# Four transfers of a turned score unit: one block of keys from all 128 partitions in place of a quarter of the queries from 32

## The chip, the cores and the metric

The kernel runs on one core of a Trainium2 chip. It is measured in device microseconds of one execution: the median of three runs before the change is 1908.62 us (1905.71 to 1908.88). Instructions go to five engines, each with its own queue in order: PE (matmuls, with weight loads PEld beside them), DVE, ACT, POOL, and SP, which here does nothing but issue transfers. All transfers are carried by the core's 16 DMA engines.

## The reference

A gated cross attention is followed by a gated mixture of experts. With x of 32 x 112 x 256 and a context of 32 x 375 x 256, all float32:

```python
lat = layer_norm(_layernorm(x))          # 112 queries a batch
kv_input = concat([layer_norm(ctx), lat])# 375 + 112 = 487 keys
q, k, v = lat @ Wq, *split(kv_input @ Wkv)   # 16 heads of 64
attn = softmax(q k^T / 8)
x = x + tanh(g_xattn) * ((attn v) @ Wout)
gate = top 2 of 8 of softmax(xf @ gate_w), made to add up to 1
x = x + tanh(g_ffn) * sum over the two of gate * (gelu(xf @ w1 + b1) @ w2 + b2)
```

What matters here is the middle: every softmax matrix (112 queries x 487 keys, one for each of 32 x 16 heads) is computed with the queries on the partitions, and the product with v needs it with the keys on the partitions.

## The kernel before

The attention goes by units. A unit is one batch and two pairs of heads, that is four score matrices of 128 x 487; there are 128 units, and two of them (two batches, the same heads) make a period, of which there are 64 (the loop over `n` in steps, two to a period).

Each unit lies in one of three SBUF tiles `exs` of 128 partitions x 2048 floats (8 KB a partition, 1 MB in all). A partition is a query: 128 of them, as four groups `a` of 32. A partition's 2048 floats are four blocks `k` of 512 floats, and a block holds, for both pairs, four chunks of keys and both heads, 32 keys `r`: key number c * 128 + k * 32 + r.

The way of a unit, with its lines:

- `scores` (L536) multiplies q and k into PSUM banks, DVE takes the row maxima (L546), and `exps` (L555) writes the exponentials from ACT into the unit's `exs` tile. As there are three tiles, unit n + 3 is written over unit n, once that one has been sent.
- `norm` (L566, L569) divides by the sums, on ACT, and `turn_blocks` (L574) turns every 32 x 32 square in place on DVE, once for each pair.
- Squares are now turned, but still stand where they stood. `send_blocks` (L580) writes the unit to a DRAM tile `turned` of four blocks k x 32 rows x four groups a x 512 floats, in four transfers issued by SP, 256 KB each. In DRAM the squares stand in the order that the product needs.
- `take_blocks` (L587) reads the whole of `turned` back in one transfer of 128 partitions x 8 KB into `exT`, of which there are two buffers. It waits on SP for the four transfers of its unit.
- `attend` (L600) multiplies v and `exT` on PE, and ACT takes the result out of PSUM (L617).

The order is written out by hand, for every engine alike (a manual schedule, with a small table `PLAN` for ten places of a period). In the first half of a period SP issues, at the second of five places, the two reads of `exT` for the units that were sent a period ago; at the fourth place it issues the four transfers of the next period's first unit, and at the second place of the late half those of its second unit. `attend` of a period stands at the start of the next one. Between them SP issues all else: loads of x and of the context (`load`, L274 and L278; a context tile goes in two transfers, of 112 and of 13 rows), pieces of the expert weights that are summed ahead (`piece_in`, `piece_out`, L1375 to L1419), rows of the output (L651). SP works in order: a transfer that has to wait holds all that stand behind it.

After the 64 periods come the experts (`hidden_pair`, `second_pair`, `run`), which don't use `turned`.

Of the kernel before, what the change touches and what calls it, by code (L numbers as in the profile page):

```python
# [23 lines left out]
def kernel(  # L24
# [59 lines left out]
    KTB, EXB, ETB = 4, 3, 2  # L84
# [18 lines left out]
    QB, QW, Q = 4, 32, S // 4  # L103
# [17 lines left out]
    turned = [dram.tile([QB, QW, QB, 2 * NCK * 2 * QW], F32, name=f"turned_{n}") for n in range(4)]  # L121
# [70 lines left out]
    if True:  # L192
# [313 lines left out]
        exs = [const.tile([P, QB, 2, NCK, 2, QW], F32, name=f"ex_{n}") for n in range(EXB)]  # L506
# [68 lines left out]

        def send_blocks(n, eng=nc.sync):


            for a in range(QB):
                eng.dma_start(  # L580
                    turned[n % 4][:, :, a, :].rearrange("k j n -> j k n"),
                    exs[n % EXB][a * QW : (a + 1) * QW].rearrange("j k q c h r -> j k (q c h r)"),
                )

        def take_blocks(n):
# [938 lines left out]
        norm(1, 0)  # L1524
        turn_blocks(0, 1)
        send_blocks(0)
        units[0, 1][6]()
        norm(1, 1)
        turn_blocks(1, 0)
        weight_sums(0, 2)  # L1530
        units[0, 1][1]()
        turn_blocks(1, 1)
        send_blocks(1)
        units[1, 0] = seven(1, 0, 0)
        for kv, k in PROLOGUE:
# [17 lines left out]
        for n in range(LAST):  # L1553
# [17 lines left out]
            def step(what, period=period, beside=beside, qn=qn):  # L1571
                s, p = int(what[1]), int(what[-1])
                if what[0] == "q":
                    for j in qn:
                        q_unit(j // NG, j % NG + NG * s)
                elif what[0] in "kv":
                    at = beside[what[0]]
                    if at[1] < (UNITS, UNITS // 2)[at[0]]:
                        if at not in units:
                            units[at] = seven(*at)  # L1580
                        units[at][p - 1]()
                elif period + 1 < UNITS:
                    s += 2 * (period + 1)
                    if what[0] == "n":
                        norm(s, p)
                    elif what[0] == "t":
                        turn_blocks(s, p)
                    else:
                        send_blocks(s)
# [24 lines left out]
            k = n - 44  # L1614
# [116 lines left out]
        r, _ = route_parts(g, nc.vector)  # L1731
# [130 lines left out]
```

## Time and profile before

| | |
|---|---|
| median of three runs | 1908.62 us (1905.71 to 1908.88) |
| the profiled execution: its own time | 1907.72 us |
| its span, first to last instruction | 1905.9 us |
| PE busy | 1876.3 us, 98% of the span |
| DVE, ACT, POOL busy | 1353.5, 1136.4, 992.5 us |
| SP's transfers, packet time as a share of 16 engines | 73.6%, 413.31 MB |
| transfers of L580: first and last issue | 34.0 and 1468.8 us, 512 of 256 KB |
| reads of `exT`, L587 | 128 of 1024 KB |

The profile tells of one execution. Each instruction has a start and a duration; a wait is put down to the semaphore that came last. "DMA share" is the mean busy share of the 16 DMA engines, "GB/s" what they moved together; the one by the other gives the rate at which a busy engine works. The transfers' packets are recorded with their sizes but without the number of the engine that carried them. A transfer's landing shows as increments of its semaphore; how many increments each transfer gave can be counted in the trace, between its issue and the next wait for the same semaphore.

### The profile page before, as it was taken

What the parts mean: (1) busy time and instruction counts of PE and PEld (TensorE: products, weight loads), DVE (VectorE), ACT (ScalarE), POOL (GpSimd) and SP (SyncE); (2) the same over time, 40 slices, a digit from 0 to 9 for tenths busy, and PEclk for the clock granted to TensorE, in tenths of its full rate; (3) what the DMA queues carried; (4) which work ended last, traced back from release to release, by engine and by line L of the source; (5) the groups of instructions that cost most, each with busy time, mean ns of one, the idle gap of its engine ahead of it and who ended that gap; (6) DMA issues with size and microseconds to landing.
All of it is one profiled execution on the core that took longest, in us unless ns stands there. A gap on an engine that the chain in (4) does not pass through costs nothing. (4 is left out here: it accounts for less than half of the span.)

```text
span 1905.9 us, 38258 instructions
## 1 busy us (share of the span) xinstructions
PE 1876.3 (98%) x12560; PEld 1433.5 (75%) x12560; DVE 1353.5 (71%) x2868; ACT 1136.4 (60%) x2718; POOL 992.5 (52%) x1475
## 2 busy tenths in 40 slices
PE   8999999999999999999999999999999999999998
PEld 4667777677777676777676777677677999999887
DVE  6787878787877878787878787878776477844111
ACT  5767666666776666667766666666756334434333
POOL 6433333435445746585556655753334588877212
PEclk9999999999999999999999999999999999999999
DMA  7777766767788888798979898896668786897872
GB/s 202 193 229 209 214 196 198 205 182 205 226 227 265 253 246 251 230 280 250 271 224 284 233 268 242 252 265 195 198 184 256 244 240 180 245 336 232 231 205 46
DMA packets 261049, 433.23 MB, mean 227 GB/s; under 512 B 30728, under 2 KB 149072, under 8 KB 244464
## 3 DMA queue, kind: packets, MB, share of 16 engines
q1 hardware_dynamic: 247232, 413.31, 73.6%
q0 software_dynamic: 11328, 15.33, 4.2%
q10 hardware_dynamic: 2288, 2.12, 0.4%
q8 instruction: 101, 1.65, 0.3%
q14 instruction: 100, 0.82, 0.1%
HBM read 301.37 MB, written 172.28 MB: 249 GB/s over the span
## 5 line engine op out<-in xcount | busy, mean ns | idle before, releaser
L555 ACT ACTIVATE ex<-bank,nmx 128x512 f32<-128x512 f32 x512 | 343.6, 697 | 85.7 <-DVE nmx L546 85.2
L569 ACT ACTIVATE ex<-ex,rc 128x512 f32<-128x512 f32 x512 | 342.7, 721 | 76.1 <-DVE rc L566 75.4
L546 DVE TENSOR_REDUCE nmx<-bank 128x1 f32<-128x487 f32 x512 | 298.6, 655 | 85.9 <-PE bank L536 83.6
L574 DVE STREAM_TRANSPOSE ex<-ex 128x1024 f32<-128x1024 f32 x256 | 314.9, 1230 | 19.5 <-ACT ex L569 15.7
L487 POOL TENSOR_TENSOR vv<-tmpv,vv 128x512 f32<-128x512 f32 x64 | 82.1, 1282 | 404.1 <-ACT vv L475 403.4
L536 PE MATMUL bank<-kT,qTs 64*128 64x487 f32 x1024 | 236.3, 588 | 3.0 <-DVE kvT L365 1.7
L600 PEld LDWEIGHTS bank<-exT,vv 128*64 128x64 f32 (+1 forms) x4096 | 198.9, 137 | 30.9 <-issue 22.6
L600 PE MATMUL bank<-exT,vv 128*64 128x112 f32 (+1 forms) x4096 | 213.0, 261 | 2.3 <-DMA exT<-turned 1.6
L617 ACT COPY outT<-bank 128x256 f32<-128x256 f32 (+3 forms) x160 | 40.0, 314 | 263.9 <-PE bank L600 258.8
L434 PE MATMUL bank<-tT,wkv_s 128*128 128x487 f32 x378 | 186.3, 575 | 0.5 <-ACT ex L555 0.5
L439 PE MATMUL bank<-wkv_s,tT 128*128 128x256 f32 x768 | 186.7, 379 | 0.0
L439 PEld LDWEIGHTS bank<-wkv_s,tT 128*128 128x128 f32 x768 | 144.8, 190 | 43.3 <-issue 21.4
L1164 POOL DMA_INDIRECT out_dram<-y,xs x60 | 93.5, 1558 | 154.0 <-DVE y L1191 77.9
L536 PEld LDWEIGHTS bank<-kT,qTs 64*128 64x128 f32 x1024 | 98.8, 187 | 99.2 <-issue 69.9
L1405 POOL TENSOR_TENSOR piece<-piece 128x128 f32<-128x128 f32 x256 | 116.9, 457 | 89.7 <-DMA piece<-in_L_ffn_w_dram 78.3
L439 PE MATMUL bank<-wkv,kvT 128*128 128x256 f32 x512 | 132.0, 380 | 0.8 <-ACT ex L555 0.6
L439 PEld LDWEIGHTS bank<-wkv,kvT 128*128 128x128 f32 x512 | 94.6, 190 | 50.5 <-issue 33.9
L484 DVE TENSOR_TENSOR kT<-bank,kT 128x487 f32<-128x487 f32 x189 | 120.8, 640 | 14.0 <-POOL kT L487 7.5
L434 PE MATMUL bank<-kvT,wkv 128*128 128x487 f32 x252 | 130.1, 598 | 0.0
L484 DVE TENSOR_TENSOR vv<-bank,vv 128x512 f32<-128x512 f32 x192 | 128.2, 668 | 1.8 <-POOL vv L487 0.2
L1219 ACT ACTIVATE h<-h,b 128x256 f32<-128x256 f32 x160 | 66.1, 495 | 91.9 <-DVE h L1230 53.2
L373 PEld LDWEIGHTS bank<-kvT,wq_sb 128*128 128x128 f32 x512 | 96.2, 188 | 28.9 <-issue 17.0
(296 smaller groups left out, 3718.2 us busy)
## 6 DMA issues: line engine op xcount, KB each, us to landing
turned<-ex SPq DMA_DIRECT2D x512, 256.0 KB
exT<-turned SPq DMA_DIRECT2D x128, 1024.0 KB
w<-in_L_ffn_w_dram SPq DMA_DIRECT2D x132, 256.0 KB
w_s<-ws SPq DMA_DIRECT2D x80, 256.0 KB
w_t<-ws SPq DMA_DIRECT2D x80, 256.0 KB
w_b2x<-in_L_ffn_w_dram SPq DMA_DIRECT2D x38, 512.0 KB
ws<-piece SPq DMA_DIRECT2D x64, 256.0 KB
cin<-in_ctx_dram SPq DMA_DIRECT2D x32, 336.0 KB
```

The source lines that it names most:

```text
L373: nc.tensor.matmul(ps, lhsT=wq_sb[:, k, i * P : (i + 1) * P], rhs=kvT[g][:, k, :, SC:NK], start=(k == 0), stop=(k == KD - 1),)
L434: nc.tensor.matmul(ps, lhsT=w[:, 0, i * P : (i + 1) * P], rhs=x[:, :NK], start=True, stop=True)
L439: nc.tensor.matmul(ps[:, c, :], lhsT=x[:, (2 * h + c) * P : (2 * h + c + 1) * P], rhs=w[:, 1, i * P : (i + 2) * P], start=True, stop=True,)
L484: nc.vector.tensor_tensor(v[o], ps, v[r], ALU.add)
L536: nc.tensor.matmul(ps[:, :NK], lhsT=qT[b // 2, i][r, b % 2].rearrange("p a i -> p (a i)"), rhs=kT[b, i][r, :], start=True, stop=True,)
L546: nc.vector.tensor_reduce(nmx[b, i][:, j : j + 1], pss[b, i][j][:, :NK], AX.X, ALU.max, negate=True)
L555: nc.scalar.activation(exs[n % EXB][:, :, p, :, j, :], ps[j].rearrange("p (c k r) -> p k c r", c=NCK, r=QW), AF.Exp, bias=nmx[b, i][:, j : ...
L569: nc.scalar.mul(t, t, rc[:, j : j + 1])
L574: nc.vector.transpose(t, t)
L600: nc.tensor.matmul(ps[y * DH : (y + 1) * DH, r, x * S : (x + 1) * S].rearrange("p (a i) -> p a i", a=QB), lhsT=vv[j // 2, c // 2][:m, c % ...
L1164: add = nc.gpsimd.indirect_dma_start(out=outf, out_offset=bass.IndirectOffsetOnAxis(ap=xs[t][:, b, D + 1 : D + 2].bitcast(I32), axis=0), i ...
L1405: nc.gpsimd.tensor_tensor(o, l, r, op) for o, l, r, op in ops
```

## The change

`send_blocks` still issues four transfers of 256 KB from SP, at the same place and behind the same waits. Before, transfer `a` carries the 32 partitions of group a whole, four blocks of 2 KB from each. Now transfer `k` carries one block of 2 KB from each of 128 partitions. What lies in DRAM at the end is the same, and so is `take_blocks`.

```diff
         def send_blocks(n, eng=nc.sync):
 
-
-            for a in range(QB):
+            for k in range(QB):
                 eng.dma_start(
-                    turned[n % 4][:, :, a, :].rearrange("k j n -> j k n"),
-                    exs[n % EXB][a * QW : (a + 1) * QW].rearrange("j k q c h r -> j k (q c h r)"),
+                    turned[n % 4][k].rearrange("j a n -> a j n"),
+                    exs[n % EXB][:, k].rearrange("p q c h r -> p (q c h r)"),
                 )
```

In the built program a transfer before has the counts 32 x 4 x 512 on both sides. After, the SBUF side counts 128 rows of 512, and the DRAM side 4 x 32 x 512: the outermost count is the group a, with 512 floats from one to the next, then the row j. One line fewer stands in the file, so all lines behind L578 have numbers that are smaller by one. The order of the instructions of every engine is the same in both programs.

## The prediction

> **What bounds the kernel now.** I read the page's busy times first, then its slices, then the attention stage alone, then what SP waits for.
>
> ```profile
> PE 1876.3 (98%) x12560; PEld 1433.5 (75%) x12560; DVE 1353.5 (71%) x2868; ACT 1136.4 (60%) x2718; POOL 992.5 (52%) x1475
> ...
> DMA  7777766767788888798979898896668786897872
> ...
> q1 hardware_dynamic: 247232, 413.31, 73.6%
> ```
>
> PE is busy for 98% of the span, in all forty slices. The DMA row is the second thing to see: 60 to 90% of all sixteen engines' time is taken in nearly every slice, so transfers have cover, but not much.
>
> The windows of the trace, first the whole stage in which L580 is issued, then three short stretches (columns: stretch, length, busy time of PE, PEld, DVE, ACT, POOL, clock, DMA share, GB/s):
>
> ```profile
> 34.00:1470.00 1436.00, 1430.30 (x9103) 1018.04 (x9101) 1130.83 (x2345) 958.66 (x2273) 725.31 (x1139) 1.00 0.80 231
> 56.00:57.50 1.50, 1.50 (x10) 1.33 (x9) 1.50 (x4) 1.38 (x4) 0.77 (x1) 1.00 0.99 198
> 58.50:59.50 1.00, 1.00 (x20) 0.88 (x20) 1.00 (x2) 0.82 (x2) 0.92 (x2) 1.00 0.99 291
> 48.00:49.50 1.50, 1.50 (x9) 1.32 (x8) 0.90 (x3) 1.50 (x7) 0.00 (x0) 1.00 0.97 410
> ```
>
> In the stage PE lacks 1436 - 1430.3 = 5.7 us, and the clock is granted in full. The 64 periods take 1436 / 64 = 22.4 us each, and a DMA engine is busy for 0.80 x 22.4 = 17.9 us of that: 4.5 us are free. The short stretches give the rate of one busy engine (GB/s / 16 / share). At 56 us only one quarter of a unit is on its way out at a time: 12.5 GB/s. At 58.5 us, with several quarters in flight, 18.4. At 48 us only `exT` comes in: 26.4. The whole stage has 18.0.
>
> SP's own waits in that stage, and its order in one period:
>
> ```profile
> SPq L580 <- DVE ex L574: 545.5, 89, 12.6
> SPq L587 <- DMA turned<-ex: 41.3, 33, 2.7
> ```
>
> ```profile
> 624.65 2.86 SPq L580 DMA_DIRECT2D turned<-ex  x4
> 627.61 1.45 SPq L1419 DMA_DIRECT2D ws<-piece  x1
> 629.61 4.23 SPq L580 DMA_DIRECT2D turned<-ex  x4
> ...
> 638.37 0.92 SPq L587 DMA_DIRECT2D exT<-turned  x2
> ...
> 645.93 3.06 SPq L580 DMA_DIRECT2D turned<-ex  x4
> ```
>
> SP waits for DVE, so sends leave as soon as their unit is turned; the reads wait 41.3 us in all for the sends to land. The sends have landed about when SP comes to the reads, 638.37 - 633.84 = 4.5 us after the last of eight was issued.
>
> **The change, part by part.**
>
> *How many engines carry a transfer.* This decides all. A transfer's semaphore must go up by 16. Counted in the trace, the 13-row loads of the context (L278) go up in 14 steps in 29 of 32 cases, and the four 2-row loads at the start (L1428) in 3 steps: one for each row, and one step for what is missing. Transfers whose outermost count is 32 (L580), 64, 112 or 128 go up in 16. So engines get whole entries of the outermost dimension, and with fewer than 16 entries fewer engines work. The new transfer has 4 there on the DRAM side, 128 on the SBUF side; no row of before has two different counts. I take the smaller: a group a is one entry and can't be cut, so four engines carry the transfer, each one group, 32 packets of 2 KB. I also take it that they are the same four each time; no row tells.
>
> The Trainium skill, page "DMA: Bandwidth & Descriptors", section "Why a DMA increments its semaphore by 16 and not by 1", says it outright: as many engines, 16 at most, as divide the outermost counts of both sides, and from SP the lowest-numbered ones. By it the new transfers all run on engines 0 to 3. Against it stands "SBUF — State Buffer", section "Door 1: The DMA port swizzle": 32 partitions reach 8 of 16 ports and 128 reach all. The row at 56 us agrees (198 GB/s with every engine busy, against 410); were that all, a unit would leave in about half the time, and the sum would be rival 1's 1906 us; by the first page it is the 2959 us below. The 13-row load decides between them here.
>
> *The busiest engines.* In a period two units leave, 8 x 262,144 bytes = 2.10 MB; a quarter of it, 524 KB, now goes through each of the four engines, where it was 131 KB. At 26.4 GB/s that is 19.9 us, at 12.5 GB/s 41.9 us. I take 18.4 GB/s, 28.5 us: the stretch at 58.5 us is nearest, as there more than one quarter is read at once, which the four engines will do too, each in a quarter of its own, two at a time in partitions that may get in each other's way.
>
> *All else on these engines.* The stage moves 231 GB/s x 1436 us = 332 MB, of which 512 x 0.262 = 134 MB are sends. The other 198 MB are spread over sixteen engines: 193 KB an engine and period. At 26.4 GB/s 7.3 us, at the stage's mean of 18.0 10.7 us; I take the middle of the rates, 22 GB/s, 8.8 us, as the twelve other engines get out of the way.
>
> *Where the queue runs dry.* SP issues the second read of `exT` only when the second unit of the period before has landed, and behind this read stand the loads, the pieces and the next sends. The first read, which waits for the first unit alone, covers some of that. Least 0; at most 4 us, about the 4.5 us that pass now between the last send and the reads; I take 1.5, an estimate nearer to the lower end since the first read is queued already.
>
> *The waits that this makes.* Three: the reads on SP (L587), longer by what the four engines are late; with them all that SP has behind them. ACT's exponentials (L555) of unit n + 3, which are written over unit n, now wait for a transfer. Behind that wait stand ACT's copies out of PSUM (L475, L617) and `norm` (L569), which DVE's `turn_blocks` and so the next sends need. PE's scores and products come behind those: the 22.4 us of compute are cover for the DMA engines up to 22.4 us and no further. Four engines with 28.5 + 8.8 + 1.5 = 38.8 us a period are the bound. PE then idles for 16.4 us in each.
>
> *Costed at nothing.* SP issues as many instructions; each may take longer for its new shape (the 512 took 407 us in all, 0.8 us each). SP waited 545.5 us for DVE, which hides even half as much again. DVE, ACT, POOL and PE do the same work. The experts after 1470 us send nothing of the kind.
>
> *Sum.* 64 x (38.8 - 22.4) = 1050 us on the profiled execution: span 1905.9 + 1050 = 2956, its time 1907.7 + 1050 = 2958; it lay 0.9 us below the median of the runs, so 2959. With all lower ends 19.9 + 7.3 + 0 = 27.2 us a period, 1908.6 + 64 x 4.8 = 2216; with all upper ends 41.9 + 10.7 + 4 = 56.6 us, 4097.
>
> **The rivals.**
>
> 1. *Sixteen engines after all.* If the 128 rows of the SBUF side set the number, all sixteen work, and their rate moves from 12.5 towards 26.4 GB/s. The mechanism is a send in half the time, at L580, and what it can give back is what PE lacks in the stage, 5.7 us, so 1903; more likely 2 or 3 us of it, 1906, since the longest wait of PE there is 1.7 us and for DVE. For it: the row at 56 us. Against it: the 13-row and 2-row loads. It decides from the point where each of the four has 16 steps. This is the case on the other side.
>
> 2. *Four engines, but another four for each transfer.* Then every engine carries one group of one block, as many bytes as before; a transfer takes 32 packets in a row where it took 8 (at 12.5 GB/s 5.2 us in place of 1.3), but four run beside each other. The reads have 4.5 us before SP comes to them, so at most a microsecond a period comes through, and PE's order has most of a period to spare: 1905 to 1920. Nothing in the rows of before speaks for or against it.
>
> 3. *Four engines, and the pairs out of each other's way.* The engines read different partitions and stay apart: 26.4 GB/s, 19.9 + 8.8 + 1.5 = 30.2 us, 1908.6 + 64 x 7.8 = 2408. For it: a busy engine can do 26.4. Against: this is the rate of reads of 8 KB a row, and the sends have 2 KB.
>
> 4. *Four engines in step.* 12.5 GB/s throughout: 41.9 + 8.8 + 1.5 = 52.2 us, 3816. For it: the row at 56 us. Against: there all sixteen draw on the same 32 partitions.
>
> **How the numbers follow.** My forecast, four fixed engines at a rate in between, 0.65; rival 3 0.15; rival 4 0.07; rival 1 0.08; rival 2 0.05. The range leaves out rivals 1, 2 and 4 (0.20) and holds the others, 50 us or so wider than rival 3 below, and above to a period of 48.2 us: 2350 to 3560. The forecast's own range, at 22 and at 15 GB/s, is 23.8 + 10.3 = 34.1 and 35.0 + 10.3 = 45.3 us a period: 2657 to 3374. A change under 0.2%, 4 us, can't be told from none. Slower: 0.87 of the four-engine cases and 0.01 of rival 2; same: 0.04 and 0.04 of rivals 2 and 1; faster 0.04. Even at all lower ends a four-engine case is 300 us slower.
>
> **What would show it.** Right: each L580 transfer's semaphore goes up in few steps, 4 and one, not 16; in the stage the DMA share falls to about four tenths ((28.5 / 4 + 8.8) / 38.8) and the bytes to 332 MB / 2483 us = 134 GB/s; SP waits for turned<-ex at L587 by hundreds of microseconds; ACT L555 waits for a transfer; PE's share is near 63%. Wrong: 16 steps and PE at 98% (rival 1), or few steps and the old time (rival 2). A busiest engine that isn't the bound would show as PE waits that don't repeat every period.

## The result, and the profile after

The changed kernel takes 2391.8 us (median of four runs, 2383.7 to 2402.4) against 1908.3 us (now the median of four runs of the kernel before): 1.254 times the time before, 95% interval 1.249 to 1.259. The forecast was 2959 us in a range of 2350 to 3560: the right side and the right bound, but a loss of 1050 us where it is 484. Rival 3, with 2408 us, is the one that came.

The profiled execution took 2383.7 us. Its page, the parts of busy times, slices and queues:

```profile
span 2381.9 us, 38258 instructions
PE 2027.8 (85%) x12560; PEld 1528.4 (64%) x12560; DVE 1359.6 (57%) x2868; ACT 1145.5 (48%) x2718; POOL 988.5 (41%) x1475
...
DMA  5544444444455555565555555555544567689783
...
q1 hardware_dynamic: 241088, 413.28, 51.7%
```

PE is down from 98% to 85%, and the DMA engines are less busy than before, 4 to 5 tenths in the attention, while the kernel is slower. Nothing in the sixteen engines' mean looks like a bound. The windows show what is hidden in that mean (stretch, length, busy times of the five engines, granted clock, DMA share, GB/s); first the stage, then two stretches in which sends are under way, in the second alone, in the first with a few other packets:

```profile
34.00:1952.00 1918.00, 1587.06 (x9124) 1117.13 (x9123) 1139.32 (x2355) 968.23 (x2274) 722.89 (x1145) 0.92 0.52 174
816.00:818.00 2.00, 2.00 (x28) 1.92 (x24) 0.62 (x2) 0.00 (x0) 1.77 (x3) 0.60 0.27 104
848.00:850.00 2.00, 2.00 (x25) 2.00 (x23) 1.46 (x3) 0.00 (x0) 1.80 (x4) 0.50 0.26 102
```

A share of 0.26 is four engines of sixteen (0.25) and a little. SP issued four sends between 810.53 and 814.74 us and four more from 817.54 us on, so several are queued at once; if each went to engines of its own, the share would be near 1. They all stand in line for the same four. The rate of one busy engine is 104 / 16 / 0.27 = 24.1 GB/s in the one stretch, 24.5 in the other.

Two counts in the trace say the same. Every one of the 512 sends makes its semaphore go up in 5 steps, four and one; before, 464 of 512 counted 16 up to the next issue on the same semaphore, and the rest fewer, as that issue came between. And of the 1919 us from the first send to the end of the last, fewer than four packets are under way in 25 us, exactly four or five in 1051 us: the four engines are hardly ever short of work. The 65,536 packets of 2 KB of the sends took 1434 us for each of four engines, 22.4 us a period; what is left of the 1919 us, 485 us or 7.6 us a period, is a remainder: all other traffic on these engines, and the little time in which they had nothing to do. Together 30.0 us a period, where it was 22.4.

That it is the same four each time, and not a queue that carries one send after the other, shows in transfers that run on all sixteen engines. The loads of the weights' pieces (L1374, 63 of 64 seen with all 16 steps) have twelve steps by 3.7 us after their issue and the last four at 6.0 to 8.7 us, in the median; before, the sixteen came evenly between 3.5 and 5.4 us. So four engines are late with their shares and twelve are not.

The waits, SP's and then all engines', and PE's first group:

```profile
SPq L586 <- DMA turned<-ex: 354.7, 117, 8.9
```

```profile
POOL piece L1404 <- DMA piece<-in_L_ffn_w_dram: 428.9, 29, 23.4
...
ACT ex L555 <- DMA turned<-ex: 141.3, 44, 5.7
PEld bank L599 <- DMA exT<-turned: 135.1, 63, 6.1
PE bank L599 <- DMA exT<-turned: 124.9, 65, 5.4
```

All three waits that were forecast are there: SP in front of the reads (41.3 us before), ACT in front of an `exs` tile that is not yet sent, and PE behind the reads. POOL's wait for the weights' pieces, 78.3 us before, shows the same: a quarter of each of these transfers goes through the four.

### The profile page after: what moved, and what is told of

Read it like the earlier page. It is cut to its first block, busy times and chain, and to the rows that moved or that the text cites. A ratio compares the mean times of both kernels' runs of the same rounds, so it can differ in the third digit from the quotient of the medians.

```text
span 2381.9 us, 38258 instructions
## 1 busy us (share of the span) xinstructions
PE 2027.8 (85%) x12560; PEld 1528.4 (64%) x12560; DVE 1359.6 (57%) x2868; ACT 1145.5 (48%) x2718; POOL 988.5 (41%) x1475
## 5 line engine op out<-in xcount | busy, mean ns | idle before, releaser
L599 PE MATMUL bank<-exT,vv 128*64 128x112 f32 (+1 forms) x4096 | 286.9, 308 | 135.6 <-DMA exT<-turned 124.9
L599 PEld LDWEIGHTS bank<-exT,vv 128*64 128x64 f32 (+1 forms) x4096 | 259.9, 168 | 179.7 <-DMA exT<-turned 135.1
L439 PE MATMUL bank<-wkv,kvT 128*128 128x256 f32 x512 | 152.9, 426 | 84.9 <-ACT ex L555 84.8
L434 PE MATMUL bank<-tT,wkv_s 128*128 128x487 f32 x378 | 193.8, 596 | 32.9 <-ACT ex L555 32.9
L439 PE MATMUL bank<-wkv_s,tT 128*128 128x256 f32 x768 | 212.6, 419 | 1.4 <-ACT ex L555 1.4
L439 PEld LDWEIGHTS bank<-wkv,kvT 128*128 128x128 f32 x512 | 101.4, 210 | 154.0 <-ACT ex L555 121.5
L439 PEld LDWEIGHTS bank<-wkv_s,tT 128*128 128x128 f32 x768 | 163.6, 215 | 54.1 <-issue 23.1
L484 DVE TENSOR_TENSOR tmpk<-bank,kT 128x487 f32<-128x487 f32 x63 | 41.9, 665 | 270.6 <-ACT kT L475 250.1
```

Source lines behind the costliest of these rows:

```text
L434: nc.tensor.matmul(ps, lhsT=w[:, 0, i * P : (i + 1) * P], rhs=x[:, :NK], start=True, stop=True)
L439: nc.tensor.matmul(ps[:, c, :], lhsT=x[:, (2 * h + c) * P : (2 * h + c + 1) * P], rhs=w[:, 1, i * P : (i + 2) * P], start=True, stop=True,)
L484: nc.vector.tensor_tensor(v[o], ps, v[r], ALU.add)
L599: nc.tensor.matmul(ps[y * DH : (y + 1) * DH, r, x * S : (x + 1) * S].rearrange("p (a i) -> p a i", a=QB), lhsT=vv[j // 2, c // 2][:m, c % ...
```

## Experiments

Theory A: a send is carried by as many engines as the outermost count of its DRAM side, four, the same each time, and these four are the bound. Theory B: a block from 128 partitions is slow as a pattern. Theory D: a transfer on few engines lands late, and each such landing costs, whatever the bytes.

**The same block from 128 partitions, on sixteen engines.** DRAM keeps the order of the partitions, so that both sides count 128 rows of 512; the reads put the groups in order, in four transfers of 32 partitions. The first two lines declare the DRAM tile in that order.

```diff
-    turned = [dram.tile([QB, QW, QB, 2 * NCK * 2 * QW], F32, name=f"turned_{n}") for n in range(4)]
+    turned = [dram.tile([QB, QB, QW, 2 * NCK * 2 * QW], F32, name=f"turned_{n}") for n in range(4)]
...
-                    turned[n % 4][k].rearrange("j a n -> a j n"),
+                    turned[n % 4][k].rearrange("a j n -> (a j) n"),
...
-            nc.sync.dma_start(
-                exT[n].rearrange("p a q c h r -> p (a q c h r)"),
-                turned[n % 4].rearrange("k j a n -> (k j) (a n)"),
-            )
+            for k in range(QB):
+                nc.sync.dma_start(
+                    exT[n][k * QW : (k + 1) * QW].rearrange("j a q c h r -> j a (q c h r)"),
+                    turned[n % 4][k].rearrange("a j n -> j a n"),
+                )
```

> Four sends of one block from all 128 partitions, with 128 rows on the DRAM side too; the groups are put in order by the reads, four a unit. Theory A (what the change costs is that only four engines carry a send, as many as the outermost count of the DRAM side): sends land in 16 steps, the DMA share in the stage is below 0.80, and the time is 1900 to 1915 us. Theory B (a block from 128 partitions is what costs, as a pattern): about 2390 us. If the outgoing rate of a busy engine is 24 GB/s or more here, the 12.5 and 18.4 GB/s of before were due to 32 partitions and not to sixteen engines at once.

Measured: 1919.7 us, 1.0062 times the time before (1.0047 to 1.0077), and 16 steps a send. Theory B falls: the SBUF side is the changed kernel's, to the byte, and 472 of the 484 us are gone. The order on the DRAM side is not slow as a pattern either: a busy engine of the changed kernel has the 24.1 to 24.5 GB/s above. The windows of this run, two with sends under way and one with reads:

```profile
56.00:57.50 1.50, 1.50 (x7) 0.95 (x6) 1.47 (x6) 1.38 (x4) 0.08 (x1) 1.00 0.68 253
58.50:59.50 1.00, 1.00 (x10) 0.58 (x10) 1.00 (x3) 0.97 (x4) 0.92 (x2) 1.00 0.76 283
...
66.00:68.00 2.00, 1.89 (x6) 0.99 (x8) 1.99 (x8) 1.20 (x3) 0.00 (x0) 0.65 1.01 226
```

A busy engine sends at 253 / 16 / 0.68 = 23.3 GB/s, in the second stretch too. That is a little under the 24 GB/s set ahead, and not every engine is busy there; the next run has 25.9 GB/s with nearly all of them busy. So the 12.5 and 18.4 GB/s of before were not a matter of how many engines write at once: they belong to sends that each draw on 32 partitions. The third line has the counterpart: reads into 32 partitions at a time, in packets of 2 KB, run at 14.0 GB/s, where reads into 128, in packets of 8 KB, ran at 26.4. Taking a quarter of the partitions costs about half the rate, in either direction. The Trainium skill's "SBUF — State Buffer", section "Door 1: The DMA port swizzle", gives 32 partitions half of the ports that 128 have, and the measured rates agree.

The expected 1900 to 1915 us was missed by 5 us, and the DMA share of the stage is 0.86, where less than 0.80 was expected: the reads lost more than the sends gained. The stage itself takes as long as before (PE busy 1429.7 of 1436 us, against 1430.3). The last period's product starts 5.5 us later and ends 9.0 us later; in front of it SP takes 6.6 us to issue eight reads, where two took 0.85 us. That the reads make the 12 us is likely from these times; no run shows it apart.

**One send of whole partitions**, 128 x 8 KB, and the four reads.

> One send of 128 partitions x 8 KB, both sides in the same order, and four reads a unit. Theory A: 16 steps, 1900 to 1915 us, like the run before it; with a quarter of the sends to issue, SP is freer. Theory B has nothing to say against sends of whole partitions and expects about 1908 us too; this run tells whether anything is to be had on the side of the reads.

Measured: 1922.4 us, 1.0073 (1.0053 to 1.0092), above the expected 1915 too. With a quarter of the sends to issue, it is no faster than the run before it: issuing the sends is not what either of them pays for; both have the eight reads a period. A stretch with its sends alone:

```profile
56.00:57.50 1.50, 1.50 (x10) 1.30 (x9) 1.50 (x4) 1.38 (x4) 0.70 (x1) 1.00 0.95 393
```

Sixteen engines that send from 128 partitions have 393 / 16 / 0.95 = 25.9 GB/s each, in packets of 8 KB, where the sends from 32, in packets of 2 KB, had 12.5 at a share of 0.99. The size of the packets is little of that: four engines had 24.1 to 24.5 with 2 KB.

**The dose.** The first 1, 2 or 3 of the four blocks are sent the new way, the others by groups of 32 partitions as before. With 2:

```diff
-            for k in range(QB):
+            for k in range(2):
                 eng.dma_start(
                     turned[n % 4][k].rearrange("j a n -> a j n"),
                     exs[n % EXB][:, k].rearrange("p q c h r -> p (q c h r)"),
                 )
+            for a in range(QB):
+                eng.dma_start(
+                    turned[n % 4][2:, :, a, :].rearrange("k j n -> j k n"),
+                    exs[n % EXB][a * QW : (a + 1) * QW, 2:].rearrange("j k q c h r -> j k (q c h r)"),
+                )
```

> One block of four is sent the new way (four engines), the other three by groups of 32 partitions as before (16 engines). Theory A, rate of the four engines: 2 x 32 packets of 84 ns (5.4 us) + three quarters of the 7.1 us of before (5.3 us) + 7.7 us of all else = 18.4 us a period, below the 22.4 us of compute: 1905 to 1925 us. Theory D (each new send lands late and what waits for it pays, whatever the bytes on the engine): a quarter of the 484 us, about 2030 us.

> Two blocks the new way, two as before. Theory A: 10.8 + 3.6 + 7.7 = 22.1 us a period, just at the 22.4 us of compute: 1910 to 1990 us. Theory D: half of the 484 us, about 2150 us.

> Three blocks the new way, one as before. Theory A: 16.1 + 1.8 + 7.7 = 25.6 us a period, 3.2 us over the compute: 2080 to 2150 us. Theory D: three quarters of the 484 us, about 2270 us.

| blocks on four engines | median us | against before | four engines' work a period, us | 64 x (that - 22.4) |
|---|---|---|---|---|
| 0 | 1908 | | | |
| 1 | 1936.2 | +28 | 5.6 + 7.9 + 7.6 = 21.1 | below 0 |
| 2 | 2043.3 | +135 | 11.2 + 5.2 + 7.6 = 24.0 | +102 |
| 3 | 2219.8 | +311 | 16.8 + 2.6 + 7.6 = 27.0 | +294 |
| 4 (the change) | 2391.8 | +484 | 22.4 + 7.6 = 30.0 | +486 |

All three lie above what theory A expected (1925, 1990 and 2150 at most) and below theory D's 2030, 2150 and 2270. The last two columns are made afterwards, with the packets of the changed kernel (22.4 us for four blocks) and a block of before at 12.5 GB/s, 2.62 us, in place of the 18.4 GB/s that I had used. So sized, theory A gives the rise from 2 blocks on within 33 us; the last row is not a test, as its terms are from that run. The first block costs less than a third of what each later one does, which theory D does not have; a bound that is reached between one and two blocks does.

The bend is not sharp: with one block the four engines have on average less to do than PE, and 28 us are lost all the same. Periods are not alike. Before, the first send of a period follows that of the one before by 20.4 us in the shortest of the periods and by 28.4 us in the longest; the short ones have no room for 21 us of transfers, and the long ones need not give it back. The times of the sends show the unevenness; that it is the reason is not shown, as no run took it away.

**Half of the partitions a send, two engines.**

```diff
             for k in range(QB):
-                eng.dma_start(
-                    turned[n % 4][k].rearrange("j a n -> a j n"),
-                    exs[n % EXB][:, k].rearrange("p q c h r -> p (q c h r)"),
-                )
+                for h in range(2):
+                    eng.dma_start(
+                        turned[n % 4][k][:, 2 * h : 2 * h + 2].rearrange("j a n -> a j n"),
+                        exs[n % EXB][2 * h * QW : (2 * h + 2) * QW, k].rearrange("p q c h r -> p (q c h r)"),
+                    )
```

> The change with every send cut in two, each half of 64 partitions, so that the DRAM side counts 2 x 32. Theory A with the same engines each time: 3 steps a landing, DMA share about 1/8 of sixteen engines while sends alone are under way, 2 x 256 packets of 84 ns = 43.0 us + 7.7 us = 50.7 us a period, 1908 + 64 x 28.3 = 3720 us. If the two engines are others each time: 2392 us or less. If engines that read partitions of the same half get in each other's way: up to twice the 43 us, 6400 us.

Measured: 3647.9 us, 1.911 times before (1.908 to 1.915), 27.2 us more a period for the 28.3 us expected; 3 steps a landing. Two of its windows with sends alone:

```profile
60.00:62.00 2.00, 0.74 (x2) 0.65 (x3) 0.00 (x0) 2.00 (x7) 0.00 (x0) 0.50 0.13 51
...
90.00:92.00 2.00, 2.00 (x14) 1.06 (x12) 0.80 (x2) 0.69 (x3) 0.00 (x0) 1.00 0.13 51
```

A share of 0.13 with eight sends a unit in the queue: two engines, always the same two, at 51 / 16 / 0.13 = 24.5 GB/s. They read partitions of the same half, 32 each, and don't slow each other. The loads of the pieces agree: fourteen of their steps come by 3.1 us, the last two at 7.8 and 8.3 us. Rival 2, engines that change, falls for SP's transfers. The Trainium skill's "DMA: Bandwidth & Descriptors", section "Why a DMA increments its semaphore by 16 and not by 1", had it: the lowest-numbered engines, as many as divide the outermost counts of both sides. The runs show the count (5 and 3 steps) and that it is the same engines each time; their numbers are in no record.

**The sends issued by POOL.**

```diff
-        def send_blocks(n, eng=nc.sync):
+        def send_blocks(n, eng=nc.gpsimd):
```

> The change with its sends issued by POOL in place of SP. Theory A says only that a send is four engines' work; if POOL's transfers go to other engines from one to the next, the share of the DMA engines while sends are under way is well above 1/4 and the four engines are no longer the bound; POOL then pays some 1 to 1.6 us for each of 512 issues beside 725 us of its own work in the stage, so 1950 to 2300 us. If they go to the same four, 2390 us or more.

Measured: 2145.6 us, a single execution. Two stretches after the first unit's sends, and POOL's group of sends:

```profile
40.00:42.00 2.00, 1.62 (x8) 1.09 (x6) 1.68 (x3) 0.00 (x0) 1.84 (x5) 1.00 0.83 126
42.00:44.00 2.00, 1.79 (x8) 1.17 (x10) 0.75 (x2) 0.00 (x0) 2.00 (x4) 1.00 0.61 144
```

```profile
L579 POOL DMA_DIRECT2D turned<-ex x512 | 358.1, 705 | 2.8 <-issue 0.3
```

The share is 0.83 and 0.61 while hardly anything but sends can be under way: from POOL's queue they reach far more than four engines. All 512 of them land in 16 steps, so whether one such send is the work of four engines, and others for the next, or of sixteen is not shown. POOL pays 705 ns a send, less than the 1 to 1.6 us expected, 358 us in all, and SP waits 674.5 us for the sends to land. The time is within the expected range, but which of the two makes the 237 us over before is not separated. A busy engine moves only 126 / 16 / 0.83 = 9.5 GB/s in the first stretch and 14.8 in the second; why stays open.

## Why the prediction was right and wrong

*How many engines: right.* Four, the same four. The step rested on the 13-row and 2-row loads, whose semaphores go up by one step a row, and no row of before had two different counts on its two sides; 5 steps in 512 of 512 sends settle the number, and the four late steps of the pieces' loads settle that they are the same.

*The busiest engines: wrong, and this is the step that failed.* "I take 18.4 GB/s, 28.5 us: the stretch at 58.5 us is nearest." It measured 24.1 to 24.5 GB/s, 22.4 us with all packets. The reason that made the row seem near was the wrong one. I saw sixteen engines get 12.5 to 18.4 GB/s each and feared the same for four that read "in partitions that may get in each other's way". But those rows are of sends that each draw on 32 partitions with sixteen engines, and the change takes just that away; with 128 partitions a busy engine has 23.3 and 25.9 GB/s among sixteen. The trace of before had the answer in the same stretch: the median packet there took 84 ns, as in the changed kernel, against 162 ns in the stretch at 56 us, and 18.4 GB/s is the mean of fast packets and slow ones. The page on ports that I weighed beside the number of engines told of this limit; I used it for a rival and not for the rate. The reason given against rival 3, that packets of 2 KB would not reach the rate of reads of 8 KB, is worth 24 against 26.4 GB/s and no more. The term is too large by 28.5 - 22.4 = 6.1 us a period, 390 of the 567 us by which the forecast was too high.

*All else, and where the queue runs dry: 7.6 us together for 10.3*, 173 us more; how they divide is shown for the second alone. Fewer than four packets are under way for 25 us in all, 0.4 us a period and not 1.5: while SP waits, what it has already issued keeps the four engines fed. For all else there is only the remainder of some 7 us, and it does not agree with the packets: the DMA share gives 0.52 x 30.0 = 15.6 us of packets an engine and period in the mean of sixteen, and without the sends, 22.4 / 4 = 5.6 us, that is 10.0 us, more than the 8.8 forecast. Packets overlap (more than sixteen are under way for 136 us of the stage), so the sum of their times may be longer than the time they need; as they carry no engine's number, this stays open. So 390 + 173 = 563 of the 567 us are no test of the parts, since the second is what was left.

*The waits: right*, as shown. *What costs nothing: right as far as it is shown.* Each issue on SP takes longer (the 512 took 906 us for 407, with a median of 1802 ns for 691), but as the four engines hardly ever lack work, that holds nothing up. PE does the same work in more time, by its clock (last section).

*The rivals.* 1 falls with the steps, 2 with the shares of 0.26 and 0.13, 4 with the rate. 3 is the case, and its 2408 us lie 16 us above the time, in part by luck: its 19.9 us for the sends are 2.5 us too low, and its 10.3 us for the rest 2.7 us too high.

*What would show it.* The stage moves 174 GB/s for the 134 forecast, which follows from a period of 30 us in place of 38.8; its DMA share is 0.52 for 0.41, from the shorter period and the 10.0 us of other packets. PE has 85% for 63%, for the same reason and because its instructions got longer (last section).

## What to carry to other kernels

Look at the outermost count of both sides of a transfer as it stands in the built program: a view that brings a group of four to the front on the DRAM side leaves four engines to carry what looks like 128 rows, and the mean DMA share then falls while the transfers become the bound. For a transfer issued by SP, count the steps of its landing: one less than the steps, where they are fewer than 16, was the number of engines here. In a stretch with such transfers alone, the share times sixteen says the same. And where a few engines have a backlog, transfers on all sixteen land in two groups, the last steps late. Take a rate only from rows that share the limit of the case at hand; a slow row whose limit the change removes is not its nearest neighbour.

## What the runs showed of the hardware that was not expected

PE's clock came down with its idle time. Before, the stage had 1.00; the changed kernel has 0.92, and the run with two engines 0.75. One gap, in the windows of the changed kernel:

```profile
808.00:810.00 2.00, 0.00 (x0) 0.00 (x0) 0.00 (x0) 0.00 (x0) 0.61 (x2) 1.00 0.96 339
810.00:812.00 2.00, 0.00 (x0) 0.00 (x0) 0.47 (x1) 0.00 (x0) 1.92 (x4) 0.69 0.97 370
812.00:814.00 2.00, 1.76 (x16) 1.41 (x16) 1.38 (x2) 0.00 (x0) 1.81 (x3) 0.50 0.48 161
814.00:816.00 2.00, 1.48 (x16) 1.49 (x18) 0.00 (x0) 0.00 (x0) 2.00 (x2) 0.50 0.60 149
816.00:818.00 2.00, 2.00 (x28) 1.92 (x24) 0.62 (x2) 0.00 (x0) 1.77 (x3) 0.60 0.27 104
```

PE had waited 5.4 us for `exT` when its products began at 812.0 us, at a clock of 0.50 for over four microseconds. In the stage its busy time is 1587 us for 1430, with the same work. The Trainium skill's "TensorE: Matmul & The Clock Gate", Part 1, gives half the clock after an idle window of about 3.4 us, which agrees with this gap. The forecast has no such term; as the four engines hardly ever ran dry, it can have cost little here, but no run measured it apart.
